# Last layer of the last image group: units of 8, 6 and 2 rows instead of four of 4, its tables loaded earlier, and two fewer buffers for the folding tables

## The chip, the cores and the metric

The kernel runs on one core of a Trainium2 chip. The metric is device time in microseconds for one execution of the whole program. Three runs of the kernel before took 6465.73, 6466.08 and 6471.06 us; their median, 6466.08 us, is the time that the changed kernel is compared with. All times of single instructions come from one more execution, recorded by the hardware profiler.

## The reference

The input x has 16 images of 32 channels with 128 x 128 pixels, in float32. Four residual layers follow one another, each on a group-normalised x. The first is a diagonal LSTM, the second an adder convolution (sums of absolute differences), the third a spectral convolution with a Hartley transform. The fourth concerns us:

```
x = x + L0(gn(x));  x = x + L1(gn(x));  x = x + L2(gn(x));  x = x + L3(gn(x))

L3(orig):
    y = five edge operators of orig, each normalised      # 160 channels
    y = maxpool2(conv1(y))                                # 128 -> 64
    y = maxpool2(conv2(y))                                # 64 -> 32
    y = maxpool2(conv3(y))                                # 32 -> 16
    y = conv4(y)
    y = conv5(deconv1(y))                                 # 16 -> 32
    y = conv6(deconv2(y))                                 # 32 -> 64
    y = conv7(deconv3(y))                                 # 64 -> 128
    return orig * y
```

Each conv is 3 x 3 with 32 output channels; each deconv is 2 x 2 and doubles the size.

## The kernel before, in words

**Groups.** The images go in four groups of four (NG = 4), so that 4 x 32 channels fill 128 partitions. While the second layer works on all images on DVE and ACT, the later layers of the first three groups are woven into it (classes `Weave` and `After`). What is left of the third group (number 2) and the whole of the last group (number 3) run afterwards. The function `drain` emits the two generators alternately, by a planner's estimate of the time, until only the last group is left. Each engine executes its instructions in the order in which they were emitted. Loads and stores go through SP's queue, in order as well, apart from a few tables that POOL issues.

**What is special about the last group.** It has the flag `whole`: its normalised image stays in SBUF (tile `image`, 128 partitions x 132 x 132) instead of being written out and read again (`kept_image`). Its pools lie on the right side of SBUF. From the moment it is alone, `acc` hands out PSUM tiles of 512 float32 (one bank each) from two pools of four in turns, eight banks in all.

**The stages of one group in the fourth layer**, with the lines of the profile:
- `back` (lines 1273 to 1361): the end of the third layer. The tile `zi` is loaded from DRAM (line 1273), multiplied by `cas_t` (line 1292), copied out of PSUM by DVE (line 1304), multiplied again (line 1342) and added onto the image (line 1317). The loads of the image's 16 pieces (line 1279) stand in SP's queue behind those of `zi`.
- `statistics`: a Gram matrix of the image (matmuls of line 1488), from which the scales of the five edge operators come.
- The fold (lines 1625 and 1627): conv1 and the five operators are folded into one 5 x 5 convolution. Ten tables `v`, each 128 x 1440 and 720 KB, are loaded from DRAM by POOL (line 1612), scaled and summed by DVE into `wf`. The entry `e_v` of `end.buffers` says how many of these tables have a buffer; when a buffer has been used, the next table is requested.
- `conv1`: matmuls of line 1844 (32 columns, the two side edges), then of line 1871 (512 columns).
- `small_layers`, called twice: for conv2 (line 1661), then for conv3, conv4 (also line 1661) and the two composed layers deconv1 + conv5 and deconv2 + conv6 (`Composed.round`, lines 908 and 934). On the second call the tables of conv3 and conv4 (`replicated`, four DMAs each, line 342) and of the two composed layers (`Composed.loaded`, one DMA each, line 891) are loaded at its start, into the pool `e_c`. That pool lies where the pools of conv1 and conv2 lay.
- `last`: the composed layer deconv3 + conv7, and the multiplication with the image. Its table is loaded at its start, into a pool that lies where `e_c` lay.

**A round of a composed layer.** `round` works on four taps. For each it emits 16 matmuls, one for each pair of an image (`blk`) and a quarter of the rows (`j`), each on a 32 x 32 part of PE. After the third tap come the bias matmuls of line 934, which correct the edges. A float32 matmul appears in the trace as two passes, each with a weight load of its own.

**The last layer** (function `last`) turns 64 x 64 into 128 x 128. The output has four parities (even or odd row, even or odd column), and each needs a round of its own. The 64 input rows are in four quarters of 16. A unit takes 4 input rows of each quarter, so there are four units. For each row parity, two rounds of 256 columns each fill the four PSUM banks, one bank for each quarter. DVE then multiplies with the image, in place (line 1993): 128 x 512 elements, four instructions for each row parity. After both, ACT adds the mean (line 1958, four instructions of 128 x 1024), and SP stores each of the four results (line 1967, 512 KB each).

Of the kernel before, what the change touches and what calls it, by code (L numbers as in the profile page):

```python
# [11 lines left out]
ALU = mybir.AluOpType  # L12
# [480 lines left out]
def rest(nc, tc, cst, sel16, bias, m1, r1, a, d, out):  # L493


    with ExitStack() as ctx:
        sm = ctx.enter_context(tc.tile_pool(name="s1_sm", bufs=1))
        stat = sm.tile([128, B, 8, 6], F32, name="stat2")
        with tc.tile_pool(name="s1_ps0", bufs=2, space=PSUM) as ps:
            first = Differences(nc, sm, ps, cst, sel16, m1, r1, a["adder_w"], d, stat)  # L500
        bg = ctx.enter_context(tc.tile_pool(name="b_ps", bufs=4, space=PSUM))
        after = After(nc, tc, "left", sm, bg, cst, bias, a, d, stat, out)
        weave = after.weave = Weave(after.work(range(NG - 1)))
        start = len(nc.cur_bb.bb.instructions)
        with ExitStack() as front:
            first.run(tc, front, weave)
        keep_order(nc, tc, start)

        end = copy.copy(after)
        end.side, end.ps = "right", ctx.enter_context(tc.tile_pool(name="c_ps", bufs=4, space=PSUM))  # L510
        end.spare, end.whole = bg, True

        end.buffers = {"t_x": 8, "xm": 8, "xw": 4, "t_w": 6, "t_r": 8, "frames": 3, "gm": 5, "e_v": 6, "l_x": 4}
        end.weave = Weave(end.work([NG - 1]))
        end.weave.now = end.weave.base = weave.now
        end.weave.finished = B - 1
        drain(weave, end.weave)
# [445 lines left out]
class After:  # L963


    def __init__(self, nc, tc, side, sm, ps, cst, bias, a, d, stat, out):
# [3 lines left out]
        self.sm, self.scales = sm, {}  # L970
# [611 lines left out]
    def encoder(self, g, kept):  # L1582
# [3 lines left out]
        if self.whole:  # L1586
            frames = self.kept_image(kept.enter_context(self.pool("e_x")))
        y2 = self.padded(kept.enter_context(self.pool("e_y2")), 32, "y2")
# [10 lines left out]
    def first_layers(self, g, fp, frames, y2):  # L1599
# [32 lines left out]
        with self.pool("e_y1") as y1p:  # L1632
            y1 = self.quartered(y1p, 64, "y1")
            self.wc = {"conv2": replicated(nc, y1p, self.a["conv2"], 9, "w_conv2")}
            yield from self.conv1(g, y1p, frames, y1, sides, wf, b1)
            with self.pool("e_c2") as cp:
                yield from self.small_layers(cp, None, y1, y2)

    def small_layers(self, cp, rp, y1, y2):
# [3 lines left out]
        if not y1:  # L1643
            for n in ("conv3", "conv4"):
                wc[n] = replicated(nc, cp, self.a[n], 9, f"w_{n}")
            up5, up6 = self.up5.loaded(cp), self.up6.loaded(cp)
# [276 lines left out]
    def last(self, g, following_group):  # L1923
# [6 lines left out]
        with self.pool("l_y") as yp, ExitStack() as ring:  # L1930
            up, ahead = self.up7.loaded(yp), self.buffers["l_x"]
            xr, following = [], {}
            if not self.whole:
                xp = ring.enter_context(self.pool("l_x", ahead))
# [7 lines left out]
            def rows(unit):  # L1942
                if self.whole:
                    x = self.image[:, 2 : H + 2, :].rearrange("p (q r) w -> p q r w", q=4)
                    return x[:, :, 8 * unit : 8 * unit + 8, 2 : W + 2]
# [36 lines left out]
            for unit in range(4):  # L1982
                complete(unit - ahead)
                x = rows(unit)
                for pr in range(2):
                    acc = [self.acc() for _ in range(4)]
                    for pc in range(2):
                        pick = lambda q: (2 * pr + pc, 16 * q + 4 * unit, 4, 256 * pc)
                        yield from up.round(self.y6, 64, acc, pick, 16)
                    yield SUMMED  # L1990
                    for q in range(4):
                        v = x[:, q, pr::2].rearrange("p r (w b) -> p r w b", b=2)
                        nc.vector.scalar_tensor_tensor(
                            v, acc[q].rearrange("p (b r w) -> p r w b", b=2, w=64), one, v, ALU.add, ALU.mult
                        )
# [7 lines left out]
            for unit in range(4):  # L2003
# [163 lines left out]
```

## Time and profile before

| What | Time |
|---|---|
| Runs, without profiler | 6465.73, 6466.08, 6471.06 us |
| Median | 6466.08 us |
| Profiled execution | 6473.52 us |
| Its span, first to last instruction | 6471.7 us |
| Mean granted clock of PE over the span | 0.931 of full speed |
| Fold (lines 1625, 1627) | 6051.96 to 6067.5 us |
| Conv1, first matmul of line 1871 to the last | 6087 to 6301 us |
| Conv2 to deconv2 + conv6 | 6300 to 6374 us |
| Last layer, first to last matmul | 6377.66 to 6459.9 us |
| Rest, to the end of the span | 11.8 us |

Times of stages count from the start of the span. The span is 1.8 us shorter than the profiled execution's time; that execution was itself 7.4 us longer than the median. PE matmuls are pipelined and their ends are modelled, so a long busy time of PE is not the same as PE at its peak. In the chain of waits and in the idle times, "issue" is time in which an engine waited for nothing that the profile shows. DMA share is the mean busy share of the core's 16 DMA engines.

### The profile page before, as it was taken

Reading aid. Unit: us, or ns where it says so; the run is one execution under the profiler, and the core shown is the slowest. Engines: PE = TensorE matmul, PEld = TensorE weight load, DVE = VectorE, ACT = ScalarE, POOL = GpSimd, SP = SyncE. Lnnn points to the kernel's source line nnn. Section 1 sums busy time; section 2 is a strip of 40 time slices with the busy share of each in tenths; the row PEclk is TensorE's granted clock in tenths of the full one; section 3 lists DMA queues with packets and bytes.
Section 4 is the critical chain, followed back from the end, with each engine's and each line's share of the span. In section 5 each row is a group of like instructions: output and inputs, shape, how many; then the busy total and the mean of one; then the engine's idle time right before and its main releaser. Section 6 shows DMA issues by size and latency. Waiting matters only on the chain.

```text
span 6471.7 us, 275922 instructions
## 1 busy us (share of the span) xinstructions
PE 5326.5 (82%) x130160; PEld 2805.8 (43%) x130160; DVE 5455.2 (84%) x6528; ACT 5276.5 (82%) x2779; POOL 58.7 (1%) x67
## 2 busy tenths in 40 slices
PE   3689577788877879998877879998888699977696
PEld 3576233344434433334443433334344333345594
DVE  7899899999999989999999889999999899834212
ACT  3899799999999989999999879999999899702001
POOL 0000000000000000000000000000000000000000
PEclk9999899999999989999999989999999899977898
DMA  7643313121154633222455532323455522344102
GB/s 313 222 178 125 87 48 84 48 57 45 32 138 124 204 117 88 64 72 73 142 147 150 168 93 58 97 51 102 129 144 179 162 58 63 97 131 137 33 4 65
DMA packets 363701, 700.94 MB, mean 108 GB/s; under 512 B 67972, under 2 KB 216452, under 8 KB 351684
## 3 DMA queue, kind: packets, MB, share of 16 engines
q1 hardware_dynamic: 355092, 648.86, 33.6%
q0 software_dynamic: 7040, 33.80, 1.6%
q8 instruction: 1018, 16.68, 1.1%
q14 instruction: 119, 0.97, 0.1%
q10 hardware_dynamic: 432, 0.64, 0.0%
HBM read 500.46 MB, written 182.69 MB: 106 GB/s over the span
## 4 chain that ended last, share of the span: by engine, by line
PE 26%; issue 11%; DVE 8%; ACT 3%; DMA 2%; SPq 0%; POOL 0%; DVEq 0%; ACTq 0%; POOLq 0%
PE acc L1871 10%; PE acc L647 9%; DVE d_dve L760 4%; PE acc L908 3%; ACT d_act L757 2%; PE acc L1661 1%; PE acc L1488 1%; PE acc L1292 1%; DMA xm_d<-xm 0%; PE acc L1218 0%; PE acc L662 0%; DVE pooled L1764 0%; PE acc L934 0%; DMA v<-fold_d 0%; PE acc L1844 0%
## 5 line engine op out<-in xcount | busy, mean ns | idle before, releaser
L757 ACT ACTIVATE d_act<-q,neg 128x8192 f16<-128x8192 f16 (+1 forms) x630 | 4463.6, 7152 | 215.9 <-PE acc L647 197.4
L760 DVE TENSOR_SCALAR d_dve<-q,qw 128x8192 f16<-128x8192 f16 (+1 forms) x1674 | 3868.3, 2360 | 215.3 <-PE acc L647 193.1
L647 PE MATMUL acc<-d_dve,sel 128*32 128x512 f16 x26784 | 1850.6, 395 | 409.4 <-DVE d_dve L760 305.6
L647 PEld LDWEIGHTS <-sel 128*32 128x32 f16 x36864 | 983.9, 99 | 1934.0 <-issue 1265.0
L647 PE MATMUL acc<-d_act,sel 128*32 128x512 f16 x10080 | 708.5, 401 | 147.9 <-ACT d_act L757 140.8
L1871 PE MATMUL acc<-xp,wf 32*32 32x512 f32 x19200 | 725.4, 607 | 23.0 <-issue 21.5
L677 PE MATMUL acc<-q,zero 128*32 128x512 f16 x8396 | 576.7, 390 | 7.1 <-issue 7.0
L223 PE MATMUL pg<-h,wb 64*64 64x20 f32 (+15 forms) x8192 | 341.3, 304 | 61.6 <-DVE h L251 34.8
L908 PE MATMUL acc<-y,u_conv 32*32 32x256 f32 x10752 | 318.4, 435 | 60.7 <-issue 45.1
L237 ACT ACTIVATE gt<-pg,bias 128x20 f32<-128x20 f32 (+15 forms) x1024 | 331.5, 383 | 41.6 <-PE pg L223 39.7
L1871 PEld LDWEIGHTS acc<-xp,wf 32*32 32x32 f32 x19200 | 222.4, 103 | 329.2 <-issue 297.9
L677 PEld LDWEIGHTS <-zero 128*32 128x32 f16 x8396 | 243.6, 99 | 228.1 <-issue 40.6
L1789 ACT ACTIVATE y<-pooled,b 128x128 f32<-128x128 f32 x112 | 39.5, 395 | 368.3 <-DVE pooled L1764 235.0
L223 PEld LDWEIGHTS pg<-h,wb 64*64 64x64 f32 x8192 | 251.4, 150 | 136.4 <-DVE h L251 81.5
L908 PEld LDWEIGHTS acc<-y,u_conv 32*32 32x32 f32 x10752 | 157.0, 110 | 164.3 <-issue 122.8
L1871 PE MATMUL acc<-image,wf 32*32 32x512 f32 x6400 | 207.8, 605 | 0.1
L223 PE MATMUL pg<-xn,wb 64*64 64x2 f32 (+63 forms) x4096 | 184.5, 290 | 25.9 <-issue 17.9
L1871 PEld LDWEIGHTS acc<-image,wf 32*32 32x32 f32 x6400 | 184.8, 103 | 20.3 <-issue 4.6
L1488 PE MATMUL acc<-xp 32*64 32x204 f32 (+2 forms) x6432 | 174.2, 338 | 15.8 <-issue 15.8
L1905 DVE TENSOR_TENSOR acc<-acc,cut 128x8 f32<-128x8 f32 x128 | 19.4, 166 | 193.4 <-PE acc L1871 193.1
L1661 PE MATMUL acc<-y,w_conv 32*32 32x512 f32 (+2 forms) x4608 | 144.3, 481 | 30.3 <-issue 18.0
L662 PE MATMUL acc<-q,sel 32*32 32x512 f16 x4608 | 158.4, 393 | 4.0 <-issue 4.0
(242 smaller groups left out, 3725.9 us busy)
## 6 DMA issues: line engine op xcount, KB each, us to landing
q<-q_d SPq DMA_DIRECT2D x128, 536.2 KB, 10.2
xp<-xn_d SPq DMA_DIRECT2D x24, 2112.0 KB, 9.1
x_in<-in_x_dram SPq DMA_DIRECT2D x16, 2048.0 KB, 14.7
xn<-in_xs_dram SPq DMA_DIRECT2D x64, 512.0 KB, 7.0
res<-in_x_dram SPq DMA_DIRECT2D x64, 512.0 KB, 8.9
x_d<-res SPq DMA_DIRECT2D x64, 512.0 KB, 4.6
xq<-x_d SPq DMA_DIRECT2D x256, 128.0 KB, 4.4
xr<-x_d SPq DMA_DIRECT2D x256, 128.0 KB, 4.3
```

Of the source, the lines that this page charges most:

```text
L223: nc.tensor.matmul(bank[c][q][64 * pair : 64 * pair + 64, :, :width], wb[half, 4 * kind + KIND[q]].rearrange("p b o -> p (b o)"), v[half], ...
L237: nc.scalar.activation(gt[:, q, :, :n], bank[c][q][:, :, :n], AF.Tanh if q == G else AF.Sigmoid, bias=bias[:, KIND[q] : KIND[q] + 1],)
L647: self.nc.tensor.matmul(acc[k][32 * j : 32 * j + 32, :], self.sel16[:, i // 9, :], d[:, row : row + 4, c : c + W], start=first, stop=last,)
L662: self.nc.tensor.matmul(acc[k][32 * j : 32 * j + 32, :], self.sel16[rows, 8, :], q[rows, row : row + 4, kw : kw + W], start=False, stop=False,
L677: self.nc.tensor.matmul(acc[k][32 * j : 32 * j + 32, :], self.zero, q[:, :4, :W], start=False, stop=False)
L757: nc.scalar.activation(dst, src, AF.Relu, bias=self.neg[:, i : i + 1])
L760: nc.vector.tensor_scalar(dst, src, self.qw[:, i : i + 1], 0.0, ALU.subtract, ALU.max)
L908: nc.tensor.matmul(acc[blk][32 * j : 32 * j + 32, o : o + rows * n], t[part, 4 * par + tap, :], own[:, top : top + rows, left : left + n], ...
L1292: nc.tensor.matmul(pa[blk][32 * r : 32 * r + 32, 32 * o : 32 * o + 32], zi[part, 16 * oh + o, :], cst["cas_t"][part, 32 * r : 32 * r + 32] ...
L1488: nc.tensor.matmul(gram[blk][j : j + width, at : at + n], xp[part, l, 2 + j : 2 + j + width], xp[part, rows, j : j + width + 4], start=sta ...
L1661: nc.tensor.matmul(acc[blk][32 * j : 32 * j + 32, : rows * n], wc[name][part, tap, :], pick(part, blk, j)[:, tap // 3 : tap // 3 + rows, t ...
L1871: nc.tensor.matmul(acc[blk][32 * j : 32 * j + 32, :], tap_of("all", tap)[rows], xp[rows, at + apart * j + kh : at + apart * j + kh + 4, kw ...
```

## The change

There are three edits, all for the last group only (`whole`), and the text for the other groups is kept.

1. The last layer's units have 8, 6 and 2 input rows of each quarter instead of 4, 4, 4 and 4. In a unit of more than 4 rows each parity fills the four banks by itself: one round of 512 or 384 columns, then four DVE instructions on every second column of every second row of the image. The unit of 2 rows keeps the old form with half the columns. Stores take 16, 12 and 4 image rows of a quarter: 1024, 768 and 256 KB each.
2. The tables of conv3, conv4 and the three composed layers are loaded into a pool of their own, `e_w`, which is opened directly after the image's pool. In SP's queue the 11 loads therefore stand behind the stores of `z_d` and ahead of the loads of `zi` and of the image.
3. `e_v` goes from 6 to 4.

In the instruction order of the two built programs, the rest is the same on every engine but for one place: around line 1292 the scheduler puts 23 `zi` matmuls behind two rounds of group 2 instead of between them, and 20 of the 128 matmuls of line 1342 directly behind the `zi` block, ahead of group 2's last layer. DVE's instructions of line 1317 follow this order.

```diff
-        end.buffers = {"t_x": 8, "xm": 8, "xw": 4, "t_w": 6, "t_r": 8, "frames": 3, "gm": 5, "e_v": 6, "l_x": 4}
+        end.buffers = {"t_x": 8, "xm": 8, "xw": 4, "t_w": 6, "t_r": 8, "frames": 3, "gm": 5, "e_v": 4, "l_x": 4}
...
         if self.whole:
             frames = self.kept_image(kept.enter_context(self.pool("e_x")))
+            cp = kept.enter_context(self.pool("e_w"))
+            self.wc = {n: replicated(nc, cp, self.a[n], 9, f"w_{n}") for n in ("conv3", "conv4")}
+            self.ups = [up.loaded(cp) for up in (self.up5, self.up6, self.up7)]
...
-            self.wc = {"conv2": replicated(nc, y1p, self.a["conv2"], 9, "w_conv2")}
+            self.wc = {**self.wc, "conv2": replicated(nc, y1p, self.a["conv2"], 9, "w_conv2")}
...
         if not y1:
-            for n in ("conv3", "conv4"):
-                wc[n] = replicated(nc, cp, self.a[n], 9, f"w_{n}")
-            up5, up6 = self.up5.loaded(cp), self.up6.loaded(cp)
+            if not self.whole:
+                for n in ("conv3", "conv4"):
+                    wc[n] = replicated(nc, cp, self.a[n], 9, f"w_{n}")
+                self.ups = [up.loaded(cp) for up in (self.up5, self.up6)]
+            up5, up6 = self.ups[:2]
...
-            up, ahead = self.up7.loaded(yp), self.buffers["l_x"]
+            up, ahead = self.ups[2] if self.whole else self.up7.loaded(yp), self.buffers["l_x"]
+            units = [(0, 8), (8, 6), (14, 2)] if self.whole else [(4 * unit, 4) for unit in range(4)]
...
-                    return x[:, :, 8 * unit : 8 * unit + 8, 2 : W + 2]
+                    return x[:, :, 2 * units[unit][0] : 2 * sum(units[unit]), 2 : W + 2]
...
             def store(x, unit, q):
-                to = self.out.offset + g * 4 * CHW + (32 * q + 8 * unit) * W
-                nc.sync.dma_start(bass.AP(self.out.tensor, to, [[HW, 128], [W, 8], [1, W]]), x[:, q])
+                first, count = units[unit]
+                to = self.out.offset + g * 4 * CHW + (32 * q + 2 * first) * W
+                nc.sync.dma_start(bass.AP(self.out.tensor, to, [[HW, 128], [W, 2 * count], [1, W]]), x[:, q])
...
-            for unit in range(4):
+            for unit, (first, count) in enumerate(units):
                 complete(unit - ahead)
                 x = rows(unit)
-                for pr in range(2):
+                for par in range(4) if count > 4 else ():
+                    acc = [self.acc() for _ in range(4)]
+                    yield from up.round(self.y6, 64, acc, lambda q: (par, 16 * q + first, count, 0), 16)
+                    yield SUMMED
+                    for q in range(4):
+                        v = x[:, q, par // 2 :: 2, par % 2 :: 2]
+                        p = acc[q][:, : 64 * count].rearrange("p (r w) -> p r w", w=64)
+                        nc.vector.scalar_tensor_tensor(v, p, one, v, ALU.add, ALU.mult)
+                        weave.dve += 0.75
+                for pr in range(2) if count <= 4 else ():
                     acc = [self.acc() for _ in range(4)]
                     for pc in range(2):
-                        pick = lambda q: (2 * pr + pc, 16 * q + 4 * unit, 4, 256 * pc)
+                        pick = lambda q: (2 * pr + pc, 16 * q + first, count, 64 * count * pc)
                         yield from up.round(self.y6, 64, acc, pick, 16)
                     yield SUMMED
                     for q in range(4):
                         v = x[:, q, pr::2].rearrange("p r (w b) -> p r w b", b=2)
-                        nc.vector.scalar_tensor_tensor(
-                            v, acc[q].rearrange("p (b r w) -> p r w b", b=2, w=64), one, v, ALU.add, ALU.mult
-                        )
+                        p = acc[q][:, : 128 * count].rearrange("p (b r w) -> p r w b", b=2, w=64)
+                        nc.vector.scalar_tensor_tensor(v, p, one, v, ALU.add, ALU.mult)
                         weave.dve += 0.75
```

More of the change, by code (lines that the diff above doesn't have):

```diff
@@ L969, in __init__ @@
         self.spare, self.banks, self.whole = None, 0, False
-        self.sm, self.scales = sm, {}
+        self.sm, self.scales, self.wc = sm, {}, {}
         self.buffers = {"t_x": 4, "xm": 3, "xw": 2, "t_w": 3, "t_r": 4, "frames": 2, "gm": 3, "e_v": 3, "l_x": 2}
@@ L2002, in last @@
                 yield -16.0
-            for unit in range(4):
+            for unit in range(len(units)):
                 complete(unit)
```

## The prediction, as made before the result

> **What bounds the kernel now.** The change acts on the last of four groups of images, and what sets the end there is one chain. I read the page first (shares, the slices, the DMA queues), then the chain of waits, then the timelines and windows of the stages that the edits touch. By the page DVE is the busiest engine, but that is an average: its row of slices falls to 3, 4, 2, 1, 2 in the last five, where PE has the work.
>
> ```profile
> PE 5326.5 (82%) x130160; PEld 2805.8 (43%) x130160; DVE 5455.2 (84%) x6528; ACT 5276.5 (82%) x2779; POOL 58.7 (1%) x67
> ...
> q8 instruction: 1018, 16.68, 1.1%
> ```
>
> Queue 8 (packets, MB, share of 16 engines) is PE's own instruction stream: 130160 matmul passes and as many weight loads are 260320 instructions; over 1018 packets that is 256 each, and 16.68 MB over them is 64 bytes each. So PE's code arrives in blocks of 256. The timeline of PE while it works on tiny matmuls shows what a block costs. First a stretch without other DMA traffic, then one where 8 MB of image are being loaded:
>
> ```profile
> 6072.04 1.53 PE L1844 MATMUL acc<-sides,wf 32*32 32x32 f32 x128 [2.23 <-issue]
> 6075.79 0.27 PE L1844 MATMUL acc<-sides,wf 32*32 32x32 f32 x3 [2.21 <-issue]
> ```
> ```profile
> 5816.53 1.54 PE L1292 MATMUL acc<-cw,zi 32*32 32x32 f32 x128 [3.00 <-issue]
> 5821.37 1.53 PE L1292 MATMUL acc<-cw,zi 32*32 32x32 f32 x128 [3.31 <-issue]
> 5826.76 1.53 PE L1292 MATMUL acc<-cw,zi 32*32 32x32 f32 x128 [3.85 <-issue]
> ```
>
> 128 passes and their 128 weight loads are one block. PE runs it in 1.53 us, then waits for "issue". The period is 6075.79 - 6072.04 = 3.75 us (3.74 below): 14.6 ns an instruction. Beside the image load it is 4.8 and 5.4 us, on average 36% more. The chain and the windows show the same wait in the last layer (lines 908 and 934):
>
> ```profile
> 6323.46 1.68 DMA w_conv<-in_conv_dram
> ...
> 6374.40 3.12 DMA u_conv<-up_d
> ...
> 6459.89 0.74 DVE image L1993
> 6460.66 2.20 ACT image L1958 x2
> ```
> ```profile
> 6121.00:6296.00 175.00, 174.98 (x5510) 163.55 (x5517) 22.05 (x67) 5.25 (x13) 0.00 (x0) 1.00 0.02 4
> ...
> 6377.60:6460.00 82.40, 62.01 (x2624) 43.51 (x2624) 19.22 (x29) 12.88 (x12) 0.00 (x0) 0.85 0.28 81
> 6460.00:6471.70 11.70, 0.00 (x0) 0.00 (x0) 2.60 (x4) 4.29 (x4) 0.00 (x0) 0.54 0.59 179
> ```
>
> In these windows PE comes first, then PEld, DVE, ACT, POOL, the granted clock, the DMA share and GB/s. Conv1 (512 columns a matmul) fills PE wholly at clock 1.00; the last layer (256 columns) fills 62 of 82 us at clock 0.85. Its 2624 passes and 2624 loads are 20.5 blocks; at 3.74 us they need 76.7 us even if PE took no time. I conclude that the last layer is bound by the arrival of instructions, not by columns. Then comes a tail of 11.8 us (PE's end 6459.87 to 6471.7) with no PE.
>
> [...]
>
> **The change, part by part.** The profiled execution took 6473.52 us with a span of 6471.7, so 1.8 lie around it; the median shown is 6466.08. Differences are worked out on the span and taken off the median.
>
> *Units of 8, 6, 2 rows (last layer).* A round is 4 taps x 16 matmuls and 16 bias matmuls, 80, each of 4 instructions (two passes, two loads). Before: 4 units x 4 rounds x 80 + 32 for the edges = 1312 matmuls, 5248 instructions (the window's 2624 + 2624). After: 12 rounds, 992 matmuls, 3968 instructions, 15.5 blocks. Columns stay the same. Five blocks go: 5 x 3.74 = 18.7 us. Is PE itself then the bound? 512 columns: conv1's 174 taps took 175.8 us, 1.01 us a tap of 64 instructions, which arrive in 0.93; 16 such taps and four bias sets (at most 0.45 each) are 18.0 us, against 19.6 for the unit's 1344 instructions. About even, so fetch keeps it. 384 columns lie below (0.76 by columns), 128 more so. Stores slow the fetch: 8.4 MB leave in all, at 290 GB/s (the DMA view of the last four). Before, three of four units (6.3 MB, 21.7 us) left beside PE; at 36% more per block a loaded us is worth 0.26 us of fetch, so 76.7 + 5.7 = 82.4, against 82.2 measured (6377.66 to 6459.87), which supports the model. After, 7.3 MB (25.3 us) leave beside PE: 57.9 + 6.7 = 64.6: some 20 us for the unit of 8, 22.5 for each of the others. Gain 17.6 us; bounds 15 (stores slow it more, or a cold clock at the start) and 20 (15.7 ns an instruction, as before on average, gives 62.2).
> DVE: 32 instructions of 744 ns become 32 of 512 or 384 elements, less eight of 256. Four take 3.0 us, a round 4.7 or more: hidden, and with eight banks a round waits only for the one before last. Uncovered it would cost 3 us once. The new form steps by two in SBUF; line 1775 also does, and takes 479 ns for 256 elements[...]: no surcharge. ACT: a row of 1024 took 1.14 us; 2048 about 2.2, four 8.8, inside the next unit.
>
> *Tail.* Before: first DVE 0.74, ACT 1.14, then 2.1 MB at 290 GB/s. After: 256 elements 0.48, ACT on 512 about 0.62; 1.05 MB in 3.6 us instead of 7.2; the other latencies (some 2.4 us) as before: 7.1 instead of 11.8, gain 4.7 (3 to 6: no store of 256 KB is in the trace; 512 KB landed in 3.3 to 5.7 us). The 3.1 MB of the middle unit need 10.9 us after a start 3.5 us behind its last matmul, and are gone before the last unit's 22.5.
>
> *Tables loaded early.* Conv3 waited until 6325.27 for w_conv, issued at 6323.46 when the inputs were ready: gain 1.8 (up to 4 if the shorter pause of 3.2 us spares the clock, 0.70 there). The last layer waited until 6377.66 for u_conv, but the copies of its edge rows on DVE end only at 6376.67: those are late next, so 1.0, not 3.1.
> The 11 issues (8 of 36 KB, 3 of 400 KB) now stand on SP ahead of zi and image. They wait for the same z_d stores as zi did, some 0.45 us an issue: zi is issued 5 us later, lands near 5806 instead of 5801 at the latest; PE's main need is at 5812.5. Image, xr and group 2's table shift by 5 us as well: the table was there at about 5831 and is needed at 5851, xr at 5860. All hidden; with zi beyond 5812 each us would count. But 1.5 MB more pass there, 5 us at 290 GB/s, beside PE's fetch: 5 x 0.26 = 1.3 us lost (0 to 3).
>
> *Order.* In the instruction order of the two builds one thing differs ahead of the tail: 20 of the matmuls of line 1342 now stand directly behind the zi block, and so wait for its DVE copies (3.7 us) and for banks, with group 2's last layer queued behind. PE stands some 8 us, a block or two arrives meanwhile, and 2.7 us of work come forward. I take 2 lost (-3 to +6: the later order is the same and part is slack).
>
> *Fold tables, 4 buffers instead of 6.* PE waits for this DVE row (19.8 us by the waits view); its work has no gap now:
>
> ```profile
> 6051.96 1.97 DVE L1625 TENSOR_SCALAR wf<-v,ops 128x1440 f32<-128x1440 f32 x3
> 6053.85 13.63 DVE L1627 SCALAR_TENSOR_TENSOR wf<-v,ops,wf 128x1440 f32<-128x1440 f32 x12
> ```
>
> POOL issued tables 6 to 9 at 6053.49, 6054.24, 6055.85 and 6057.61, each once a buffer was free, and they landed 4.7 to 6.0 us later. Now these slots carry tables 4 to 7, and 8 and 9 come after. With 1.66 and 1.75 us a table: table 4 is there at 6058.2 (wanted 6057.26), 5 at 6060.0, 6 at 6061.6, 7 at 6063.6, 8 (issued 6060.2) at 6066.0, 9 at 6067.9; the row ends at 6069.7 instead of 6067.5. Loss 2.2 (1 to 5).
>
> Sum: -17.6 - 4.7 - 1.8 - 1.0 + 1.3 + 2.0 + 2.2 = -19.6: span 6452.1, median **6446.5**. The parts together leave 6438 to 6453.
>
> **Rivals.** *The clock drops in the wide rounds.* For it: 0.55 in parts of the last layer. At half clock a 512-column tap takes 2.02 us, one of 384 1.52: the first two units take 34 + 26 instead of 42.5, 18 us lost, 6464. Against it: conv1 ran at 1.00 throughout, and wide rounds leave fewer pauses. *The front costs more.* One v load took 11.9 us to land; if two waits in the fold row cost 4 more each and the order and SP parts reach their upper ends (+6), 14 are lost: 6460. For it: these are the least certain costs; against: the long landing was beside five other loads. *Slower: DVE's stepped form.* If reading and writing SBUF in steps of two costs DVE more, its four instructions pass the 5.2 us mean of a wide round at 1.3 us each; over eight rounds the gain is gone at 1.9 us each, and at four times the row's 744 ns the loss is 8 x (11.9 - 5.2) = 54, less 20: 6500. Against it: line 1775. *It doesn't do what it says*, if the fetch is not the bound and columns are: then rounds cost as before by column, only tail and waits gain, near 6464; the two stretches of tiny matmuls and the model's 82.4 speak against it, and I count it with the first rival.
>
> **Chances.** Forecast 0.79 (all of it faster), clock or columns 0.08 and front 0.09 (both within 0.2%), DVE 0.04. About 0.2% (12.9 us) is what a measurement of this kernel can tell from no change. So faster 0.79, same 0.17, slower 0.04. The range takes in the forecast's bounds and much of the front rival: 6436 to 6459.
>
> **What would show it.** The last layer some 64 us long with 1984 passes; the unit of 8 near 20 us with PE almost full at clock 1; the others still with "issue" between bursts; about 7 us from the last matmul to the end; conv3 some 1.8 us after conv2's last pool; gaps of 1 us in the fold row before tables 4 and 8. I am wrong if rounds of 384 and 128 columns differ much in time, if the clock falls, or if the layer before (at 6323) already starts over 5 us late.

## The result, and the profile after

The changed kernel takes 6444.54 us, the median of five runs (6431.92 to 6450.13); the kernel before took 6465.73 us beside it (five runs, 6458.02 to 6471.06). By the medians it is 21.2 us faster, 0.33%; the ratio over all these runs is 0.9963, with a 95% interval of 0.995 to 0.9975. The prediction was 19.6 us faster.

The profiled execution took 6444.54 us, with a span of 6442.8. That is 28.9 us less than the span of before. I split both spans by landmarks in the timelines of DVE and SP. A stretch runs from the start of one named instruction to the start of the next, but the fold row ends with the end of its last instruction. "The last multiplication" is the start of the last four of DVE's instructions on the image.

| Stretch | Before, us | After, us | Difference | Predicted |
|---|---|---|---|---|
| Start to the first store of `z_d` (same code in both) | 5788.0 | 5780.3 | -7.7 | 0 |
| Front: to the first fold instruction | 263.9 | 269.8 | +5.9 | +3.3 |
| Fold row on DVE | 15.5 | 19.1 | +3.6 | +2.2 |
| Conv1, conv2, to the last pools of conv2 | 252.8 | 250.6 | -2.2 | 0 |
| Conv3, to its first pool | 14.9 | 9.1 | -5.8 | -1.8 |
| To the last eviction of the layer before the last | 39.0 | 38.9 | -0.1 | 0 |
| Last layer, to its last multiplication | 85.6 | 67.3 | -18.3 | -18.6 |
| Tail | 11.8 | 7.7 | -4.1 | -4.7 |

The first line is chance: over all profiled runs of this case that moment lies between 5768.9 and 5788.7 us, in code that no kernel changed. Without it the table gives -21.1 us. The other stretches vary as well between profiles of kernels that don't differ there: conv1 and conv2 took 252.8 us in the profile of before and 249.1 to 251.6 us in the thirteen others, so the -2.2 us of that line is not put down to the change.

The page of the changed kernel has the rows for the instruction stream (engine, busy time, passes; queue: packets, MB, share):

```profile
PE 5302.7 (82%) x129520; PEld 2796.8 (43%) x129520; DVE 5457.9 (85%) x6536; ACT 5275.7 (82%) x2775; POOL 60.6 (1%) x67
...
q8 instruction: 1013, 16.60, 1.1%
```

640 passes and 640 weight loads are gone, and with them five packets, as counted. The windows of the changed kernel, with columns as in the prediction: the pause before conv3 and conv3 itself, then the units of 8, 6 and 2, and the tail:

```profile
6319.70:6322.60 2.90, 1.33 (x19) 0.45 (x16) 2.88 (x7) 0.57 (x2) 0.00 (x0) 1.00 0.00 0
6322.60:6328.90 6.30, 5.88 (x272) 4.14 (x272) 1.52 (x17) 0.23 (x1) 0.00 (x0) 1.00 0.01 3
...
6368.50:6390.70 22.20, 22.13 (x685) 15.03 (x695) 10.06 (x18) 0.53 (x1) 0.00 (x0) 0.92 0.02 5
6390.70:6413.30 22.60, 18.96 (x657) 11.68 (x650) 9.39 (x16) 7.75 (x4) 0.00 (x0) 0.92 0.65 188
6413.30:6435.10 21.80, 12.85 (x675) 10.30 (x664) 3.89 (x9) 6.02 (x4) 0.00 (x0) 0.67 0.51 149
6435.10:6442.80 7.70, 0.00 (x0) 0.00 (x0) 1.62 (x4) 2.57 (x4) 0.00 (x0) 0.50 0.45 136
```

The three units have columns in the ratio 4 : 3 : 1 and take 22.2, 22.6 and 21.8 us. What they have in common is the number of instructions (1344, 1280 and 1344). (The unit of 8 turns out to be a case of its own; see the part on why the prediction was right.) In the unit of 2 rows PE is busy for 12.85 of 21.8 us. The chain of waits of the changed kernel names what fills the rest there:

```profile
6417.89 2.95 issue
...
6423.65 2.30 issue
...
6435.58 1.34 ACT image L1964 x2
```

What ends these waits can be read from the trace as well. PE's timeline of the changed kernel has, in the unit of 2:

```profile
6420.84 1.12 PE L908 MATMUL acc<-y,u_conv 32*32 32x128 f32 x38 [2.95 <-issue]
...
6425.95 1.76 PE L908 MATMUL acc<-y,u_conv 32*32 32x128 f32 x71 [2.30 <-issue]
```

In the same trace's records of queue 8, blocks of PE's code landed at 6419.32 and 6424.51 us, 1.5 and 1.4 us earlier. It is so every time: between the first and the last matmul of the last layer PE waits nine times for over 0.3 us, and each wait ends 1.2 to 1.5 us after such a block landed. In the kernel before there are sixteen, and each ends 1.2 to 1.6 us after a landing. None of the nine lies in the unit of 8.

The next view is DVE's timeline, first a line of the kernel before, then two of the changed kernel (start, time of the group, line, shapes, number; in brackets the idle time ahead and what ended it):

```profile
6387.08 2.73 DVE L1993 SCALAR_TENSOR_TENSOR image<-acc,l_one,image 128x512 f32<-128x512 f32 x4 [10.16 <-PE acc L908]
```
```profile
6376.24 2.74 DVE L1999 SCALAR_TENSOR_TENSOR image<-acc,l_one,image 128x512 f32<-128x512 f32 x4 [5.84 <-PE acc L908]
...
6435.06 1.66 DVE L2010 SCALAR_TENSOR_TENSOR image<-acc,l_one,image 128x256 f32<-128x256 f32 x4 [10.33 <-PE acc L908]
```

The new form, with a step of two in rows and columns, takes 2.74 us for four of 512 elements, the old form 2.73. A single instruction takes 756 ns on average in the new form and 745 in the old; four in a row overlap a little. DVE waits for PE before every round.

### The profile page after: what moved, and what is told of

Read it like the earlier page. It is cut to its first block, busy times and chain, and to the rows that moved or that the text cites. A ratio compares the mean times of both kernels' runs of the same rounds, so it can differ in the third digit from the quotient of the medians.

```text
span 6442.8 us, 274628 instructions
## 1 busy us (share of the span) xinstructions
PE 5302.7 (82%) x129520; PEld 2796.8 (43%) x129520; DVE 5457.9 (85%) x6536; ACT 5275.7 (82%) x2775; POOL 60.6 (1%) x67
## 5 line engine op out<-in xcount | busy, mean ns | idle before, releaser
L1876 PE MATMUL acc<-xp,wf 32*32 32x512 f32 x19200 | 726.2, 608 | 17.6 <-issue 17.6
L908 PE MATMUL acc<-y,u_conv 32*32 32x256 f32 (+3 forms) x10240 | 308.0, 441 | 53.6 <-issue 40.2
L223 PE MATMUL pg<-xn,wb 64*64 64x2 f32 (+63 forms) x4096 | 184.8, 291 | 25.7 <-issue 17.6
L1876 PEld LDWEIGHTS acc<-image,wf 32*32 32x32 f32 x6400 | 186.3, 103 | 18.3 <-issue 4.0
```

The lines of the kernel that those rows point to most:

```text
L223: nc.tensor.matmul(bank[c][q][64 * pair : 64 * pair + 64, :, :width], wb[half, 4 * kind + KIND[q]].rearrange("p b o -> p (b o)"), v[half], ...
L908: nc.tensor.matmul(acc[blk][32 * j : 32 * j + 32, o : o + rows * n], t[part, 4 * par + tap, :], own[:, top : top + rows, left : left + n], ...
L1876: nc.tensor.matmul(acc[blk][32 * j : 32 * j + 32, :], tap_of("all", tap)[rows], xp[rows, at + apart * j + kh : at + apart * j + kh + 4, kw ...
```

## The experiments

The runs of one batch are compared with runs of the kernel before on the same chip; its median was 6455.9 us for the first four kernels, 6448.8 for the next four and 6464.8 for the last four. Since these medians differ among themselves, I read effects from ratios and from stretches of one profile. "Front", "fold row" and so on are the stretches of the table above. Each run has one profile, so a difference of a microsecond or two in the front can be chance.

**E1: only the units** (the tables at their old place, six fold buffers).

```diff
-"e_v": 4, "l_x": 4}
+"e_v": 6, "l_x": 4}
...
-            cp = kept.enter_context(self.pool("e_w"))
-            self.wc = {n: replicated(nc, cp, self.a[n], 9, f"w_{n}") for n in ("conv3", "conv4")}
-            self.ups = [up.loaded(cp) for up in (self.up5, self.up6, self.up7)]
...
-            if not self.whole:
-                for n in ("conv3", "conv4"):
-                    wc[n] = replicated(nc, cp, self.a[n], 9, f"w_{n}")
-                self.ups = [up.loaded(cp) for up in (self.up5, self.up6)]
+            for n in ("conv3", "conv4"):
+                wc[n] = replicated(nc, cp, self.a[n], 9, f"w_{n}")
+            self.ups = [up.loaded(cp) for up in (self.up5, self.up6)]
...
-            up, ahead = self.ups[2] if self.whole else self.up7.loaded(yp), self.buffers["l_x"]
+            up, ahead = self.up7.loaded(yp), self.buffers["l_x"]
```

> The units of 8, 6 and 2 rows alone; tables loaded where they were, six fold buffers. If PE's code arrives at a fixed rate and that bounds the last layer, it takes from DVE's last copy of deconv2 + conv6 to the last matmul about 69 us (85.6 before, 67.4 in the changed kernel, and the wait for its table is back), with a tail of 7.7. Conv3 waits for its table again: 14.9 us from conv2's last pool group to its own first, clock near 0.7 (9.1 and 1.00 in the changed kernel). Stage from the z_d stores to the fold 264 us, fold 15.5 without a gap. Total about 20 us below the kernel before. If instead the last layer gained because the tables came early and spared the clock, it stays near 80 us and the total gains under 8.

Measured: 6428.73 us, ratio 0.9957 (0.9943 to 0.9972). Front 259.4, fold row 15.5, conv3 14.3, last layer 69.4, tail 7.6. So the units alone bring as much as the whole change (0.9963): -16.2 in the last layer and -4.2 in the tail. The PE timelines of E1 and of the changed kernel at the first wide round show what the early table adds:

```profile
6354.71 4.93 PE L908 MATMUL acc<-y,u_conv 32*32 32x512 f32 x87 [3.40 <-DMA u_conv<-up_d]
```
```profile
6368.57 5.79 PE L908 MATMUL acc<-y,u_conv 32*32 32x512 f32 x83 [0.87 <-ACT y L1794]
```

A wait of 3.40 us for the table becomes one of 0.87 for ACT's eviction. The last layer is 2.1 us shorter for it (69.4 to 67.3).

**E2: only the early tables and the four buffers**, with the old units.

```diff
-            units = [(0, 8), (8, 6), (14, 2)] if self.whole else [(4 * unit, 4) for unit in range(4)]
+            units = [(0, 4), (4, 4), (8, 4), (12, 4)] if self.whole else [(4 * unit, 4) for unit in range(4)]
```

> The tables loaded early and four fold buffers, with four units of 4 rows. If the parts add up as in the trace of the changed kernel: z_d to fold 270 us (264 before), fold 18.6 (15.5), conv3 9.1 (14.9), last layer 83 (85.6, a wait of 3 us less), tail 11.8: together about 1 us above the kernel before, nothing that can be told from it. If the early tables are a gain of their own as the prediction had it for the two waits (2.8 us) and more by the clock, it is 5 us faster; if the 6 us of the front were chance, also.

Measured: 6454.69 us, ratio 0.9999 (0.9991 to 1.0008): nothing. Front 268.6, fold row 17.5, conv3 8.8, last layer 84.8, tail 11.8. The zero is a sum: -6.1 at conv3 and -0.8 in the last layer are paid back by +4.7 at the front and +2.0 in the fold row (against the kernel before in its profile, whose front is the longest of the three without early tables). In this kernel PE's wait for the table of the last layer fell as in the changed kernel, from 3.44 to 0.87 us, and yet the last layer is only 0.8 us shorter than before, and no shorter than in E3 below (84.9), which has the late table. Conv3's gain is in every kernel with early tables (8.8 to 9.3 us) and in none without (14.3 to 14.9).

**E3: only the four fold buffers**, in the kernel before.

```diff
-"e_v": 6, "l_x": 4}
+"e_v": 4, "l_x": 4}
```

> Four fold buffers instead of six, nothing else. If landing times of the fold tables set the row, it takes 18.6 us instead of 15.5, with gaps before table 4 and the last tables, and the total is 3 us above the kernel before; z_d to fold stays at 264 us and conv3 at 14.9. If the gaps in the changed kernel came from something else that the change brought, the row stays at 15.5.

Measured: 6456.1 us, ratio 0.9999 (0.9991 to 1.0008). The fold row takes 17.5 instead of 15.5 us; the front is 260.8, as without early tables. 2 us are there in the profile, and too small for the ratio.

**E4: units of 8 and 8**: the same columns in fewer instructions (2688 for PE instead of 3968; the trace has 1344 passes).

```diff
-            units = [(0, 8), (8, 6), (14, 2)] if self.whole else [(4 * unit, 4) for unit in range(4)]
+            units = [(0, 8), (8, 8)] if self.whole else [(4 * unit, 4) for unit in range(4)]
```

> Changed kernel with two units of 8 rows: the same columns, 8 rounds of 80 matmuls instead of 12 (2624 instead of 3968 instructions). If the arrival of code is the bound, the last layer falls from 66.5 us to 44 to 46 (first to last matmul); if columns and clock are, it stays near 66. The tail grows: ACT on 2048 elements 2.2 us before the first store and 4.2 MB at 290 GB/s, about 18.5 us instead of 7.7. Total by the first theory 10 us below the changed kernel, by the second 11 above.

Measured: 6425.91 us, ratio 0.9956 (0.9941 to 0.9971). The last layer takes 46.1 instead of 67.3 us: with the same columns, 32% fewer instructions take 31% less time. It is the strongest test of the fetch against columns, which can't explain it. A fixed cost of PE for each matmul could; what speaks against that is the landing of the blocks, shown above, at the end of each wait. The tail rises to 20.1 us, since the last four results are now 1 MB each. The windows of E4 are most of five rounds, then three rounds beside stores, then the tail:

```profile
6370.00:6391.40 21.40, 21.40 (x778) 14.51 (x773) 11.01 (x16) 3.74 (x2) 0.00 (x0) 1.00 0.05 13
6391.40:6410.00 18.60, 16.02 (x514) 8.84 (x500) 8.41 (x13) 4.02 (x3) 0.00 (x0) 1.00 0.75 219
6410.00:6430.10 20.10, 0.00 (x0) 0.00 (x0) 2.69 (x4) 7.73 (x4) 0.00 (x0) 0.51 0.71 209
```

Beside stores of 219 GB/s the three rounds take 6.2 us each on average, although PE's clock stays at 1.00.

**E5: the tables later**: requested after conv2's table, where the scheduler places them behind the image rows of group 2's last layer in SP's queue. PE's order is then that of the kernel before.

```diff
-            self.wc = {n: replicated(nc, cp, self.a[n], 9, f"w_{n}") for n in ("conv3", "conv4")}
-            self.ups = [up.loaded(cp) for up in (self.up5, self.up6, self.up7)]
+            self.cp = cp
...
-            self.wc = {**self.wc, "conv2": replicated(nc, y1p, self.a["conv2"], 9, "w_conv2")}
+            self.wc = {"conv2": replicated(nc, y1p, self.a["conv2"], 9, "w_conv2")}
+            if self.whole:
+                for n in ("conv3", "conv4"):
+                    self.wc[n] = replicated(nc, self.cp, self.a[n], 9, f"w_{n}")
+                self.ups = [up.loaded(self.cp) for up in (self.up5, self.up6, self.up7)]
```

> Changed kernel with the table loads written into the code of conv1; as their pool is free, the scheduler puts them in SP's queue behind group 2's xr loads, and PE's order is that of the kernel before. The stage from the z_d stores to the fold took 259 to 264 us in three kernels without early tables and 268 to 270 in three with them. If the other order of the zi and line 1342 matmuls costs it, it falls to about 263 (the 1.5 MB still pass beside PE's code, worth 1 to 3 us); if the traffic of the tables is all of the cost, it stays near 268. Fold 17.5 to 19, conv3 9.0, last layer 67, tail 7.7. Total about 5 us below the changed kernel.

Measured: 6427.65 us, ratio 0.9972 (0.9957 to 0.9987). Front 266.1, fold row 18.9, conv3 8.9, last layer 67.1. `zi` is requested 7.0 us after the first `z_d` store, as early as in the kernel before (6.5; 13.4 in the changed kernel). Yet the front stays long. The 5 us expected in the total don't show: the ratio is no lower than that of the changed kernel. More on this below.

**E6: six fold buffers** beside the rest of the change.

```diff
-"e_v": 4, "l_x": 4}
+"e_v": 6, "l_x": 4}
```

> Changed kernel with six fold buffers again, tables early. If the buffers alone set the fold row, it takes 15.5 us without gaps (17.4 to 19.1 with four), the rest stays (front 269, conv3 9, last layer 67, tail 7.7), and the total is 2 to 3 us lower. If the tables' place in memory or their traffic delayed the fold tables, gaps remain.

Measured: 6429.31 us, ratio 0.9968 (0.9956 to 0.998); the 2 to 3 us expected in the total can't be seen in it. DVE's timeline of the changed kernel in the fold, and below it the same of E6:

```profile
6050.08 1.97 DVE L1628 TENSOR_SCALAR wf<-v,ops 128x1440 f32<-128x1440 f32 x3
6051.97 3.47 DVE L1630 SCALAR_TENSOR_TENSOR wf<-v,ops,wf 128x1440 f32<-128x1440 f32 x3
6056.27 1.72 DVE L1630 SCALAR_TENSOR_TENSOR wf<-v,ops,wf 128x1440 f32<-128x1440 f32 x1 [0.83 <-DMA v<-fold_d]
...
6059.15 6.96 DVE L1630 SCALAR_TENSOR_TENSOR wf<-v,ops,wf 128x1152 f32<-128x1152 f32 x6 [1.16 <-DMA v<-fold_d]
6067.28 1.85 DVE L1630 SCALAR_TENSOR_TENSOR wf<-v,ops,wf 128x1152 f32<-128x1152 f32 x2 [1.16 <-DMA v<-fold_d]
```
```profile
6042.58 1.97 DVE L1628 TENSOR_SCALAR wf<-v,ops 128x1440 f32<-128x1440 f32 x3
6044.46 13.63 DVE L1630 SCALAR_TENSOR_TENSOR wf<-v,ops,wf 128x1440 f32<-128x1440 f32 x12
```

With four buffers the row has three gaps, 3.15 us in all, each ended by the landing of a table; with six it has none. Six buffers always gave 15.5 us (before, E1, E6 and the combination), four gave 17.4 to 19.1. The early tables and six buffers fit into SBUF together.

**E7: units of 8 and 8, the last one finished by row parity**: once both column parities of the even rows are done, ACT and the stores of those rows go ahead, as pieces of every second row.

```diff
-            def done(x, unit):
+            def done(x, unit, pr=None):
                 for q in range(4):
-                    nc.scalar.activation(x[:, q], x[:, q], AF.Identity, bias=mean)
+                    v = x[:, q] if pr is None else x[:, q, pr::2]
+                    nc.scalar.activation(v, v, AF.Identity, bias=mean)
...
+                if pr is None:
+                    to = bass.AP(self.out.tensor, to, [[HW, 128], [W, 2 * count], [1, W]])
+                else:
+                    to = bass.AP(self.out.tensor, to + pr * W, [[HW, 128], [2 * W, count], [1, W]])
...
+                    if unit == len(units) - 1 and par == 1:
+                        weave.on_act(lambda x=x, unit=unit: done(x, unit, 0))
...
```

> Two units of 8 rows; the last one is finished by row parity: after its first two rounds ACT and the stores take the even rows, after the other two the odd rows (stores in pieces of 512 bytes). The last layer stays near 46 us from DVE's last copy of deconv2 + conv6 to the last matmul (46.1 with whole rows), a little more if the stores slow PE's code. Tail: DVE 0.74, ACT 1.14, 2.1 MB at 290 GB/s: about 12 us instead of 20.1; if pieces of 512 bytes move at half the rate, about 19, and nothing is gained. Total by the first 8 us below two plain units of 8.

Measured: 6421.46 us, ratio 0.9955 (0.9941 to 0.9968). The last layer takes 45.9 us and the tail 12.6 instead of 20.1. The windows of E7 are the last rounds and the tail:

```profile
6386.00:6404.90 18.90, 16.26 (x526) 9.08 (x510) 8.49 (x13) 8.59 (x7) 0.00 (x0) 1.00 0.97 283
6404.90:6417.40 12.50, 0.00 (x0) 0.00 (x0) 2.64 (x4) 4.29 (x4) 0.00 (x0) 0.57 0.81 239
```

The first window holds the whole-block stores of the first unit (4.2 MB) and the first of the stepped ones; the second holds stepped ones alone: 239 GB/s at a DMA share of 0.81, against 209 at 0.71 in E4's tail with whole blocks, so 295 and 294 GB/s for a full share by my estimate. Whole blocks moved in packets of 512 bytes as well (the tails of the kernel before and of the changed kernel). Last layer and tail together: 97.4 us before, 75.0 in the changed kernel, 66.2 in E4, 58.5 here.

**E8 and E11: the combination** of E5, E6 and E7, run in two batches; its diff is theirs.

> Two units of 8 with the last finished by row parity, tables behind group 2's xr loads, six fold buffers. By the parts: front 263, fold 15.5, conv3 9, last layer 46 to 48, tail 12. Against the changed kernel: -5 (front), -2.5 (fold), -20 (last layer), +4 (tail): about 23 us below it, 44 below the kernel before. If the parts hide one another (PE then waits for DVE or for the stores), less than 35 below the kernel before.

> The combination once more (units of 8 and 8, the last one finished by row parity, tables behind the requests of group 2's last layer, six fold buffers), beside the changed kernel on the same chip. If its parts add up, it is 6 to 14 us below the changed kernel: about 8 from the last layer and tail together (59 against 75 less what conv3 and the start keep), 2 to 3 from the fold, 0 to 3 from the front. If the earlier difference was chance, 0 to 3.

Measured: 6416.06 us, ratio 0.9951 (0.9938 to 0.9965), and in the last batch 6432.42 us, ratio 0.9942 (0.9926 to 0.9958). E8 was expected 44 us below the kernel before and is 32.7 by medians, a miss. Its fold row (15.5), conv3 (9.1), last layer (46.9) and tail (12.2) came as expected; only its front (266.9 for 263) did not. By profiles alone, from the first store of `z_d` on, E8 is 24.3 us shorter than the changed kernel, where 23 were expected; why the medians show less is open. E10 below, the changed kernel in the same batch as E11, has 6446.78. The combination is thus 14.4 us faster than the changed kernel by medians, 0.24% by the two ratios. By the stretches of E10 and E11, the last layer and tail give -15.9 and the fold row -3.2, while the front gives +0.6.

**E9: the tables directly behind the image's loads.**

```diff
-            self.wc = {n: replicated(nc, cp, self.a[n], 9, f"w_{n}") for n in ("conv3", "conv4")}
-            self.ups = [up.loaded(cp) for up in (self.up5, self.up6, self.up7)]
+            self.cp = cp
...
                     nc.sync.dma_start(self.image[:, 2 + row : 10 + row, 2 : W + 2], src)
+                self.wc = {n: replicated(nc, self.cp, self.a[n], 9, f"w_{n}") for n in ("conv3", "conv4")}
+                self.ups = [up.loaded(self.cp) for up in (self.up5, self.up6, self.up7)]
```

> The changed kernel with the 11 table loads put directly behind the 16 loads of the image in SP's queue instead of ahead of zi. PE's order around lines 1292 and 1342 is then to be read from the trace. Theory (the 7 us at the front are the order, about 4, and the transfers that delay the image, about 3): zi and the image are requested early again, so the image's part should go; the time from the first z_d store to the fold should be 263 to 267 us, against 269.8 in the changed kernel and 261.4 in the mean of the kernels without early tables. Rival (only the place of the transfers ahead of zi costs): 261 to 262. Rival (only the order costs, the transfers nothing): about 265.5 if the order is that of the changed kernel. Total 2 to 5 us below the changed kernel.

**E10: the changed kernel once more.**

> The changed kernel once more, unedited, on the same chip as the others of this batch: 16 to 26 us below the kernel before. It shows how far stage times of one kernel vary between two profiles: front 267 to 272 us, fold row 17 to 20 us, last layer 66 to 69 us, tail 7.5 to 8.

Measured: E9 6448.97 us, ratio 0.9971 (0.9959 to 0.9983); E10 6446.78 us, ratio 0.9966 (0.9952 to 0.998). In E9 line 1317 begins 71.9 us after the first `z_d` store, as in the changed kernel (72.6; 81.5 before), so the order is the changed kernel's. E9's front is 266.3, within what my theory gave, but its total isn't below E10's, so that part was a miss. E10's stretches are front 269.5, fold row 18.7, conv3 9.3, last layer 67.4, tail 7.7: all as in the first profile of the change, to within 0.4 us.

**E12: the bias matmuls of the last group's last layer left out** (line 934; the edges of that output lack their correction). Taps, columns and stores stay.

```diff
-            if tap != 2:
+            if tap != 2 or self.bare:
                 continue
...
+            up.bare = self.whole
```

> The changed kernel with the bias matmuls of the last group's last layer left out (line 934, 14 sets of 16; the edge correction of its output is missing). Taps, columns, DVE and ACT work and stores stay. Instructions of PE in the last layer: 3968 - 896 = 3072, 12 blocks instead of 15.5. Fetch theory: 3.5 blocks less, 13 us, and more where stores run beside it: the last layer takes 51 to 55 us instead of 67.3, the unit of 8 about 17 to 18, the units of 6 and 2 about 17 to 19 each. Column theory (a bias set costs at most 0.45 us of PE): 6 us less, 61 us, and the units of 6 and 2 stay unequal to nothing but their columns.

Measured: 6444.54 us, a single run. The last layer takes 58.6 us, between both expectations. The windows of E12 are the four rounds of the unit of 8 (the first in two parts), then the units of 6 and 2:

```profile
6376.90:6380.00 3.10, 3.06 (x36) 1.77 (x40) 1.74 (x6) 0.50 (x1) 0.00 (x0) 0.50 0.02 5
6380.00:6385.30 5.30, 5.30 (x123) 3.80 (x112) 0.00 (x0) 0.00 (x0) 0.00 (x0) 0.65 0.02 5
6385.30:6389.55 4.25, 4.25 (x149) 3.59 (x137) 2.75 (x4) 0.00 (x0) 0.00 (x0) 1.00 0.02 4
6389.55:6393.60 4.05, 4.05 (x145) 3.40 (x132) 2.77 (x4) 0.00 (x0) 0.00 (x0) 1.00 0.02 4
6393.60:6397.30 3.70, 3.70 (x137) 3.14 (x125) 2.81 (x4) 0.00 (x0) 0.00 (x0) 1.00 0.02 4
6397.30:6416.10 18.80, 14.60 (x540) 10.54 (x524) 9.49 (x16) 7.76 (x4) 0.00 (x0) 1.00 0.77 224
6416.10:6434.70 18.60, 9.36 (x491) 7.03 (x488) 3.85 (x8) 6.01 (x4) 0.00 (x0) 0.82 0.59 174
```

The units of 6 and 2 behave as the fetch has it: 2048 instructions, 8 blocks of 3.74 us and 6.6 for the stores beside them (25.3 us of them at 0.26, as in the prediction) make 36.5 by my estimate; measured 37.4. The unit of 8 doesn't: without bias, its 256 instructions a round arrive in 3.74 us, but its columns need 4 taps of 1.01 us, and at clock 1.00 the rounds took 3.7 to 4.25. There the columns became the bound: the three rounds after the first took 4.0 us on average. The first round ran at clock 0.50 and 0.65 and took 8.4 us. My expectation for E12 had forgotten both. Column theory alone fails as well: it can't make the units of 6 and 2 equal.

## Why the prediction was right, and where its terms were not

**The bound (right).** The prediction held that the last layer waits for PE's code, in blocks of 256 instructions at 3.74 us. The blocks that landed ahead of the end of each wait, the units of 6 and 2 with equal times at columns of 3 : 1, E4's fewer instructions and the last two units of E12 all show it. It does not hold for the unit of 8, as the next paragraph shows. The wait is plainest in the unit of 2, where PE was busy for 12.85 of 21.8 us.

**Units and table (right sum, two errors).** From first matmul to last multiplication I predicted 64.6 us; it was 66.5 (6368.57 to 6435.06). The 2 us lie in the unit of 8: 22.2 instead of 20. They are not the clock's doing. Windows of E10 for the same unit, first round in two parts:

```profile
6362.80:6365.00 2.20, 2.20 (x30) 0.98 (x42) 1.69 (x6) 0.46 (x1) 0.00 (x0) 1.00 0.00 0
6365.00:6369.40 4.40, 4.40 (x179) 3.43 (x166) 0.09 (x1) 0.00 (x0) 0.00 (x0) 1.00 0.04 9
6369.40:6374.40 5.00, 5.00 (x188) 3.14 (x175) 2.81 (x5) 0.00 (x0) 0.00 (x0) 1.00 0.01 3
6374.40:6380.00 5.60, 5.60 (x186) 3.17 (x167) 2.81 (x5) 0.00 (x0) 0.00 (x0) 1.00 0.03 6
6380.00:6384.50 4.50, 4.50 (x174) 3.37 (x163) 2.77 (x5) 0.00 (x0) 0.00 (x0) 1.00 0.01 4
```

Here the clock was 1.00 throughout, and the unit still took 21.7 us. After the first, a round took 5.0 us on average, against 4.67 by arrival and 4.5 by columns with the bias. The prediction had it "about even, so fetch keeps it", and that was the wrong side: PE doesn't wait for code in this unit, and its fourth round, from one start of DVE's four instructions to the next, took 4.52 or 4.53 us in all ten profiles that have such a unit with the bias: what the columns ask, and less than by arrival. So columns set the pace here, and that the three units came out equal is partly luck. The excess over the columns lies in the first and the third round (the third 5.6 us here, 5.1 to 5.9 in all ten); its cause is open. The other error goes the other way. I gave the early table 1.0 us, because the copies of the edge rows on DVE would be late next. They were not: PE's wait fell from 3.44 to 0.87 us, by 2.6, and what ended it was ACT's eviction. So -15.7 and -2.6 stand for -17.6 and -1.0 in the trace. That a shorter wait is worth its length is not shown, though: E1 puts 16.2 us down to the units and leaves 2.1 for the table, and with the old units the same shorter wait brought 0.8 us or nothing (E2).

**Conv3 (term too small).** Predicted -1.8, "up to 4 if the shorter pause spares the clock"; measured -5.8. It was both, not one or the other. The windows of the kernel before are the pause and conv3:

```profile
6320.00:6325.20 5.20, 0.72 (x8) 0.00 (x0) 4.40 (x22) 0.81 (x2) 0.00 (x0) 0.93 0.06 14
6325.20:6335.20 10.00, 9.45 (x287) 6.59 (x288) 0.00 (x0) 0.00 (x0) 0.00 (x0) 0.70 0.38 108
```

After a pause of 4.54 us (PE's timeline) conv3 ran at 0.70 for 10.0 us; in the changed kernel PE's longest wait there is 1.18 us, the clock stays at 1.00, and conv3 takes 6.3. PE was busy for 9.45 of the 10.0 us, so it was the slow columns and hardly the wait for code that took them. So with a wait of 1.8 us went some 4 more on the clock. The prediction had left room for this, and I took the lower end. How long a pause makes the clock fall is not shown: in the kernel before it was also 0.50 in the stage of line 1844, where PE's waits are 2.2 us, and 1.00 in conv1.

**Tail (right).** 7.7 for 7.1.

**Fold (term too small).** 3.6 for 2.2; the other profiles with four buffers show 1.9 to 3.3. E3 and E6 tie it to the buffers.

**Front (term too small, cause open).** Predicted +1.3 for traffic and +2.0 for the order. The fronts of all profiles, by the place of the tables:

| Tables | Kernels | Front, us | Mean |
|---|---|---|---|
| Not early | before, E1, E3 | 263.9, 259.4, 260.8 | 261.4 |
| Ahead of `zi` | after, E2, E4, E6, E7, E10, E12 | 269.8, 268.6, 268.1, 266.0, 270.8, 269.5, 269.7 | 268.9 |
| Behind the image | E9 | 266.3 | 266.3 |
| Behind group 2's rows | E5, E8, E11 | 266.1, 266.9, 270.1 | 267.7 |

Tables ahead of `zi` cost 7.5 us. By landmarks, 2.9 of them arise while DVE makes its copies of line 1304 and 4.5 while the third layer's result is added onto the image (line 1317). PE's timeline of the changed kernel shows both waits that I had named: a slow arrival beside the loads, and line 1342 waiting for the copies.

```profile
5837.00 1.55 PE L1292 MATMUL acc<-cw,zi 32*32 32x32 f32 x128 [4.88 <-issue]
...
5850.74 4.67 PE L1342 MATMUL acc<-cw,o 32*128 32x128 f32 x40 [3.69 <-DVE o L1304]
```

After E5, I took the order for the larger part. E8 and E11 don't bear that out. Behind group 2's rows, with PE's order of before, these two steps cost only 0.9 and 1.0 us more, but the time to the first copy is 3.3 us longer, in all three profiles, and some 2 us of that lie before the tables are even requested. No place gave the time back. What joins these kernels, and why their front stays 5 to 7.5 us long, wasn't settled.

**The rivals.** The clock did drop in the wide rounds (0.68 and 0.84 in the first 8 us), but the unit with the full clock was only 0.5 us shorter: 21.6 to 21.9 us in the four profiles with clock 1.00 throughout (E5, E7, E8, E10), 22.1 to 22.7 in five with a low clock at the start (the changed kernel, E4, E6, E9, E11). E1 is the exception, with 21.4 us at a low clock, after its wait of 3.4 us for the table. It dropped again in the unit of 2, to 0.67, where PE waits for code anyway. DVE's stepped form cost nothing that counts (756 ns for 745). The dearer front came half true: it and the fold cost 9.5 instead of 5.5 us. It was covered by conv3's 4 us, and the -2.2 us of conv1 and conv2 came by chance, so the total of -21.1 against -19.6 owes much to errors that cancel. Two of the signs that the prediction had named for being wrong came true as well: the clock fell, and counted from the first store of `z_d` the pause before conv3 came 7.2 us late. The first cost little, and conv3 made up for most of the second beyond its forecast.

## What to carry to other kernels

Where PE shows "issue" between bursts and stretches of unequal columns take equal time, count instructions, not columns: wide matmuls pay (E4: 32% fewer instructions, 31% less time), and so does a smaller number of bias matmuls (E12: 58.6 us instead of 67.3), until the columns of a round take as long as its code (E12, 512 columns: 4.0 us against 3.74). When the last unit is made large for this reason, let its finished rows leave early: in E4 the tail took back 12.4 of the 21.2 us that the last layer gained on the changed kernel, in E7 4.9 of 21.5. A wait of PE for data that is made shorter need not bring its length where code bounds what follows (E2: 3.44 to 0.87 us, and 0.8 us or nothing gained). A wait of 1.8 us ahead of PE can go with three times that, as conv3's 5.8 us did: with it PE's pause was 4.54 us and the clock after it 0.70, without it no wait was longer than 1.18 us and the clock stayed at 1.00.

## What the runs showed of the hardware that was not expected

- PE's code comes in blocks of 256 instructions (16 KB). Waits of PE for it ended 1.2 to 1.6 us after the block had landed (25 waits in the last layers of the kernel before and the changed kernel). The transfer of one block took 0.9 to 1.5 us there, and 0.9 to 1.4 us in the stage of line 1844, whose period of 3.74 us is thus for the most part not transfer.
- Float32 matmuls on 32 x 32 parts need some 480 columns each before columns take as long as their code. This is an estimate: a round of 64 matmuls without bias took 4.0 us at 512 columns and clock 1.00 (E12), and its 256 instructions alone take 3.74.
- A clock of 0.68 to 0.84 over the first round of the last layer cost about 0.5 us in 22; in conv3 0.70 instead of 1.00 cost about 4 in 10.
- Stores of every second row were no slower than whole blocks: 239 GB/s at a DMA share of 0.81 in E7's tail, 209 at 0.71 in E4's, which is 295 and 294 for a full share (an estimate from these windows).
